# Two SwiGLU layers in fp32 on one core: block 0's last 96 features computed at the end of its block, as a product of seven

## The chip, the core and the metric

The kernel runs on one core of a Trainium2 chip. The metric is the device time of one launch in microseconds; lower is better. All arithmetic is in fp32. TensorE is called PE below, VectorE DVE, ScalarE ACT, GpSimd POOL and SyncE SP, as in the profile.

## The reference

2048 tokens (4 x 512) of width 512 pass two residual layers, each with a layer norm before and after. The first layer keeps, token by token, only the 688 of 1376 gate values that are largest in magnitude.

```python
def layer1(x, w_gate, w_up, w_down):                 # I = 1376, H = 512
    s = silu(x @ w_gate.T)
    s = zero_the_smaller_half_by_abs(s)              # per token, k = I / 2
    return (s * (x @ w_up.T)) @ w_down.T

x = x + layernorm(layer1(layernorm(x), ...))
x = x + layernorm((silu(xn @ W_gate.T) * (xn @ W_up.T)) @ W_down.T)   # xn = layernorm(x)
```

## The kernel before, in words

**Work and stages.** The first layer takes the 16 token tiles of 128 in eight *units* of two tiles (0 to 7). The second layer takes them in four *blocks* of four tiles (0 to 3), with N = 512 tokens a block. Between the layers stand x1 rows in DRAM: each unit's output is normed, added to x and stored there, and a block loads its four tiles again (`Block.norm`: load, layer norm, four transposes on PE, copies to `xT`).

**The second layer's gate and up products.** Of the 1376 features, 1280 are taken in five *groups* (`Block.group`, PE line 849). Each group is a fast bilinear scheme of 26 products of 128x128 by 128x256, whose moving operands are signed sums of `xT` (`Block.sums`, the tiles `T` and `Ts`, 18 additions on DVE, line 277) and whose stationary operands are sums of weights made earlier. The results are gathered from PSUM by DVE (line 859) and ACT (line 863), and POOL multiplies gate by up (line 872).

**The last 96 features.** 1376 is 1280 + 96. For blocks 1 to 3 the gate and up rows of these 96 features are one product of seven (`Block.rest_sevens`, a Strassen-Winograd product over class `Seven`, PE line 210): its left operand is the seven sums `rest_left` of the weights `w_rest`, its right operand the sums `R` of `xT`, which POOL makes in four additions (`Block.rest_right`, lines 193 to 196, tiles `R` with the tag "y"). For block 0 they are computed plainly (`Block.rest`, PE line 881: two outputs, each four matmuls of 128x96 by 128x512), at the change of layers, ahead of the last unit's down product.

**The down product.** `downs` (helper lines 339 to 455) makes it for a pair or two pairs of tiles, in seven products p1 to p7 of five matmuls each (PE line 368), with the last 96 rows as single matmuls into the same banks (line 374). Its weights come as one 640 KB load for each product (`wd_p`, in three buffers). Outputs are gathered in tiles `y` (tag "y", four buffers), normed (`out_norm`: line 170 statistics, line 176 the power -1/2 on POOL, line 486 less the mean, line 488 times the scale plus `xr`), and stored.

**The change of layers.** After unit 7's products the program writes: the down product of units 5 and 6, `blocks[0].norm`, unit 7's search and transposes (`ph`, line 750), `blocks[0].sums()`, `blocks[0].rest`, the down product of unit 7, then the groups of block 0.

**What sets the order.** Every engine executes its own queue in order. The order in the queues is not the written one: a scheduler merges the steps by its own estimate of times when the program is built, and keeps to `tc.issue_after(...)` where that stands. So the order is fixed in the built program, and can be read there for both kernels. Tiles with the same tag share a ring of buffers: a new tile waits until the old one in its buffer has been read and stored. Loads and stores all pass one SP queue in order.

Of the kernel before, what the change touches and what calls it, by code (L numbers as in the profile page):

```python
# [9 lines left out]
F32 = mybir.dt.float32  # L10
BF16 = mybir.dt.bfloat16
I32 = mybir.dt.int32
AF = mybir.ActivationFunctionType
# [3 lines left out]
P = 128  # L17
# [76 lines left out]
def sandwich_kernel(  # L94
# [18 lines left out]
    nc = tc.nc  # L113
    NT, H = x.shape
    I = a_wg.shape[1]
    K = int(0.5 * I)
    assert 2 * K == I
    NH = H // P
# [7 lines left out]
    N = TB * P  # L126
# [3 lines left out]
    HF = HC * P  # L130
# [24 lines left out]
    x1 = dram.tile([NT, H], F32, name="x1")  # L155
# [5 lines left out]
    def bank(tag, nm):  # L161
        return psum.tile([P, 512], F32, tag=tag, name=nm)
# [20 lines left out]
    def stationary_sums(eng, a11, a12, a21, a22, s1, s2, s4):  # L183

        eng.tensor_add(s1, a21, a22)
        eng.tensor_sub(s2, s1, a11)
        eng.tensor_sub(a21, a11, a21)
        eng.tensor_sub(s4, a12, s2)
        return dict(p1=a11, p2=a12, p3=s4, p4=a22, p5=s1, p6=s2, p7=a21)
# [149 lines left out]
        nc.sync.dma_start(t, src)  # L339
        return t  # L340

    def downs(work, pairs, key, w_d, wr, res, dst, nm, final=False):

# [7 lines left out]
        def begin():  # L353
            tiles, left, last = pairs[len(st)]
            pa, px, py = [bank(k, f"{k}d{nm}_{tiles[0]}")[:, :H2] for k in ("pa", "px", "py")]
            ya, yb = [
                work.tile([P, H], F32, tag="y", name=f"y{nm}_{t}", bufs=4) for t in tiles
            ]
            st.append((tiles, left, last, pa, px, py, ya, yb))

# [21 lines left out]
        def p1(i):  # L382
            begin()
            product("p1", PA, i)
# [7 lines left out]
        def p7():  # L392
            product("p7", PX)
            for p in st:
                tiles, left, last, pa, px, py, ya, yb = p
                nc.vector.tensor_add(yb[:, hi], yb[:, lo], px)
                pz.append(bank("pt", f"pz{nm}_{p[0][0]}")[:, :H2])
                rest(pz[-1], p, 1, hi, True)
# [382 lines left out]
                self.tiles, lambda k, c: self.dleft[k][:, c, :], lambda i: self.hT[i][1]  # L781
            )

    def finish(units, wr):

        u = units[0]
        steps = downs(u.work, [u.pair() for u in units], "a", a_wd, wr, x, x1, u.nm)

        def p2():
            steps[-3]()  # L790
            for u in units:
                a12, s2 = u.dleft["p3"], u.dleft["p6"]
                nc.vector.tensor_sub(a12, a12, s2)

        return steps[:-3] + [p2] + steps[-2:]

    class Block:
# [73 lines left out]
                    if not left[f] and not left[2 + f]:  # L871
                        nc.gpsimd.tensor_mul(h[:, part], sg[:, part], h[:, part])  # L872

        def rest(self, w):

            n = I - 2 * HF
            nm = f"{self.nm}_{self.b}"
            ps = [bank(k, f"{k}rb{nm}")[:n, :] for k in ("pa", "px")]
            for c, t in zip(ps, w):
                for k in range(NH):  # L880
                    nc.tensor.matmul(
                        c, t[:, k, :], self.xT[k // 2][:, k % 2, :],
                        start=k == 0, stop=k == NH - 1,
                    )
            h = self.work.tile([P, N], F32, tag="junk", name=f"hTb{nm}_r", bufs=1)
            nc.scalar.activation(h[:n], ps[0], AF.Silu)
            nc.vector.tensor_mul(h[:n], h[:n], ps[1])
            self.hr = h

        def rest_right(self):  # L890

            t = [
                self.work.tile([P, 2, N2], F32, tag="y", name=f"R{self.nm}_{self.b}_{q}", bufs=4)
                for q in range(4)
            ]
            self.right = moving_sums(
                nc.gpsimd,
                *[half[:, :, cols] for half in self.xT for cols in (slice(N2), slice(N2, N))],
                *t,
            )  # L900

        def rest_sevens(self, left):

            n = I - 2 * HF
            nm = f"{self.nm}_{self.b}"
            t = self.work.tile([P, 4, N2], F32, tag="c", name=f"sgr{nm}")[:n]
            m = Seven(f"rb{nm}", left, self.right, t[:, 0, :], t[:, 1, :], t[:, 2, :])
            m.first()
            c11 = m.second()
            h = self.work.tile([P, N], F32, tag="junk", name=f"hTb{nm}_r", bufs=1)  # L910
            lo, hi = h[:n, :N2], h[:n, N2:]
            nc.scalar.activation(lo, c11, AF.Silu)
            m.third()
            nc.scalar.activation(hi, m.c12, AF.Silu)
            nc.vector.tensor_mul(lo, lo, m.c21)
            nc.vector.tensor_mul(hi, hi, m.c22)
            self.hr = h
# [32 lines left out]
    def count_bad():  # L950

        bad = small.tile([P, 1], F32, tag="bad", name="bad", bufs=2)
        nc.vector.tensor_reduce(bad, flags, AX.XY, ALU.add)
        pb = bank("pt", "pbad")
        nc.tensor.matmul(pb[:1, :1], bad, onec, start=True, stop=True)
        badi = const.tile([1, 1], I32, name="badi")
        nc.vector.tensor_copy(badi, pb[:1, :1])
        traced = nc.cur_bb.bb.instructions
        k = len(traced)
        nbad = nc.values_load(badi[0:1, 0:1], min_val=0, max_val=2 * P * NTT)  # L960
        return nbad, [i for i in traced[k:] if i.engine == mybir.EngineType.DVE]

    def layers(nm, general):
        with ExitStack() as sctx:
            wpool = sctx.enter_context(tc.tile_pool(name="w" + nm, bufs=1))
            big = sctx.enter_context(tc.tile_pool(name="big" + nm, bufs=10))
            work = sctx.enter_context(tc.tile_pool(name="work" + nm, bufs=2))

            def last_rows(w_d, layer):
                n = I - 2 * HF  # L970
                w = work.tile([P, H], F32, tag="wr", name=f"wr{layer}{nm}", bufs=1)
                nc.sync.dma_start(w[:n, :], w_d[2 * HF :, :])
                return w[:n, :]

            blocks = [Block(b, nm, big, work) for b in range(NTT // TB)]


            units = [Unit(j, nm, big, work) for j in range(NU)]
# [14 lines left out]
            for q in range(2):  # L993
                b = [
                    wu[:, 2 * r : 2 * r + 2, k * Q : (k + 1) * Q] for r in range(2) for k in (q, 2 + q)
                ]
                t = [y[:, :, ts(q, Q)] for y in (t1, t2, t4)]
                right.append(moving_sums(nc.vector, *b, t[0], t[1], b[1], t[2]))
            nbad = None
            if general:  # L1000
                wr = last_rows(a_wd, 1)
# [13 lines left out]
            else:  # L1015
                wr = last_rows(a_wd, 1)
# [3 lines left out]
                for j in range(NU):  # L1020
                    gate, up = [[] for i in range(6)], [[] for i in range(6)]
                    if j > 2:
                        steps = finish([units[j - 3]], wr)
# [26 lines left out]
                steps = finish(units[-3:-1], wr)  # L1050
# [23 lines left out]
            for tag, n in (("wg", 43), ("wu", 43), ("wus0", 10), ("wus1", 10)):  # L1074
                n = min(n, NG * NP - len(w_of))
                t = wpool.tile([P, n, P], F32, tag=tag, name=f"{tag}2{nm}")
                i = 0
                while i < n:
                    g, j = divmod(len(w_of), NP)
                    k = min(NP - j, n - i)  # L1080
# [3 lines left out]
            n = I - 2 * HF  # L1084
            t = wpool.tile([P, 7, 2, n], F32, tag="wus2", name=f"w_rest{nm}")
            w_rest = [t[:, 2 * q : 2 * q + 2].rearrange("p a b h -> p (a b) h") for q in range(2)]
            for w, w_d in zip(w_rest, (f_wg, f_wu)):
                nc.sync.dma_start(w, w_d[:, 2 * HF :].rearrange("(k p) h -> p k h", p=P))
            w_rests = [t[:, q] for q in range(4, 7)]
            if general:  # L1090
                blocks[0].sums()
            else:
                blocks[0].sums()
                blocks[0].rest(w_rest)
                for f in finish([units[-1]], wr):
                    f()
            wr = last_rows(f_wd, 2)
            for b, block in enumerate(blocks):
                last = b + 1 == len(blocks)
                for a in range(HC):  # L1100
                    block.group(a, w_of[a * NP : (a + 1) * NP])
                    block.down_sums(a)
                    if b == 2 and a == 0 and not general:
                        nbad, loads = count_bad()
                    if b and a == 1:
                        with tc.issue_after(normed[-1]):
                            block.rest_right()
                if b:
                    block.rest_sevens(rest_left)
                elif general:  # L1110
                    block.rest(w_rest)
                if b == 0:
                    blocks_w = [w[:, 2 * c : 2 * c + 2, :] for w in w_rest for c in range(2)]
                    with tc.issue_after(block.mark):
                        rest_left = stationary_sums(nc.vector, *blocks_w, *w_rests)
                if not last:
                    with tc.issue_after(block.mark):
                        for k in range(TB):
                            blocks[b + 1].norm(k)
                    blocks[b + 1].sums()  # L1120
                with ExitStack() as order:
                    if last and not general:
                        for i in loads:
                            order.enter_context(tc.issue_after(i))
                    block.finish([0, 1], wr, last)
# [43 lines left out]
```

## Time and profile before

| What | Value |
|---|---|
| median of 3 runs (lowest to highest) | 848.5 us (848.37 to 850.13) |
| the profiled execution, its time | 848.49 us |
| its span | 846.7 us, 10717 instructions |
| granted TensorE clock over the span | 0.998 |
| DVE busy | 592.4 us (70%) |
| ACT busy | 346.9 us (41%) |
| POOL busy | 178.4 us (21%) |
| DMA moved | 112.20 MB, mean 133 GB/s |

The profiled execution took 1.8 us more than its span and is level with the median. Busy time is what the profiler recorded on an engine; a row of the groups view gives a source line, the engine, the tile names, the count, the busy time and the mean of one. PE's records overlap: a matmul of fp32 leaves two records, which start 0.216 us apart at 256 columns although each lasts 0.379 us. So on PE the distance between starts is what counts. The chain of work that ended last lies on PE for 98% of the span and on DMA for 1%.

### The profile page before, as it was taken

The page shows a single profiled execution, that of the slowest core. Times are in us where ns is not written, and L with a number is a line of the kernel's source. Part 1 is how long each engine was busy: PE and PEld are TensorE (multiplying, and loading weights), DVE is VectorE, ACT ScalarE, POOL GpSimd, SP SyncE. Part 2 cuts the span into 40 slices and gives each one's busy share as a digit, 9 for nine tenths or more (in the row PEclk, how much of TensorE's full clock was granted, in tenths as well). Part 3 has the DMA queues.
Part 4 walks back from the last instruction along what each step waited for, and adds up shares of the span by engine and source line. Part 5 has one row for each costly group of instructions (what it writes and reads, how often), then busy time and mean ns, then how long its engine had stood idle before and what let it go on. Part 6 is the DMA issues. An engine that isn't in the chain of part 4 may idle for free.

```text
span 846.7 us, 10717 instructions
## 1 busy us (share of the span) xinstructions
PE 837.0 (99%) x3544; PEld 641.0 (76%) x3544; DVE 592.4 (70%) x1676; ACT 346.9 (41%) x717; POOL 178.4 (21%) x236
## 2 busy tenths in 40 slices
PE   9999999999999999999999999999999999999996
PEld 5656566767667667677868888888888888888885
DVE  5988769697887949587796665776656666476524
ACT  3356675556557573746321331133211332033300
POOL 1010000000100000000020553074503653075401
PEclk9999999999999999999999999999999999999999
DMA  9996013827424134277557002520055001530032
GB/s 338 385 355 234 1 56 102 278 75 246 137 87 160 56 125 160 71 263 275 183 186 252 1 2 74 200 93 1 2 174 185 8 1 30 205 120 1 1 99 80
DMA packets 65393, 112.20 MB, mean 133 GB/s; under 512 B 4720, under 2 KB 44784, under 8 KB 64432
## 3 DMA queue, kind: packets, MB, share of 16 engines
q1 hardware_dynamic: 65184, 111.16, 38.5%
q8 instruction: 30, 0.49, 0.2%
q14 instruction: 35, 0.29, 0.1%
q10 hardware_dynamic: 144, 0.26, 0.1%
HBM read 90.96 MB, written 20.45 MB: 132 GB/s over the span
## 4 chain that ended last, share of the span: by engine, by line
PE 98%; DMA 1%; DVE 0%; issue 0%; POOL 0%; ACT 0%; POOLq 0%
PE pg L575 18%; PE pab L849 9%; PE pxb L849 9%; PE pyb L849 8%; PE pxu L210 7%; PE pxd L368 6%; PE pxdb L368 6%; PE pyu L210 4%; PE pau L210 4%; PE padb L368 4%; PE pydb L368 4%; PE pad L368 4%; PE pyd L368 4%; PE ph L750 2%; PE pxrb L210 1%; DMA wdb_p<-in_L_ffn_W_down_dram 1%
## 5 line engine op out<-in xcount | busy, mean ns | idle before, releaser
L627 ACT ACTIVATE ja<-v,cur 128x1376 bf16<-128x1376 f32 x96 | 138.4, 1442 | 54.8 <-DVE cur L652 43.6
L575 PE MATMUL pg<-wg,xT 128*128 128x456 f32 (+1 forms) x384 | 155.2, 549 | 0.0
L575 PEld LDWEIGHTS pg<-wg,xT 128*128 128x128 f32 x384 | 72.0, 190 | 61.9 <-issue 57.2
L872 POOL TENSOR_TENSOR hTb<-sg,hTb 128x512 f32<-128x512 f32 x40 | 50.8, 1272 | 96.9 <-DVE hTb L859 90.6
L176 POOL TENSOR_TENSOR rs_o<-ve_o,nhalf 128x1 f32<-128x1 f32 x16 | 14.4, 917 | 181.0 <-DVE ve_o L174 181.0
L579 ACT ACTIVATE p<-pg 128x456 f32<-128x456 f32 (+1 forms) x48 | 26.3, 547 | 58.6 <-PE pg L575 47.9
L176 POOL TENSOR_TENSOR rs_i<-ve_i,nhalf 128x1 f32<-128x1 f32 x16 | 13.2, 829 | 152.8 <-DVE ve_i L174 58.5
L870 ACT ACTIVATE sg<-sg 128x512 f32<-128x512 f32 x40 | 23.0, 621 | 49.0 <-DVE sg L859 49.0
L210 PE MATMUL pau<-wu,xT 128*128 128x344 f32 x128 | 42.7, 452 | 0.0
L859 DVE TENSOR_TENSOR sg<-sg,pxb 128x256 f32<-128x256 f32 x80 | 33.7, 421 | 10.3 <-PE pxb L849 8.3
L859 DVE TENSOR_TENSOR hTb<-hTb,pab 128x256 f32<-128x256 f32 x60 | 25.1, 419 | 22.4 <-PE pab L849 11.0
L368 PE MATMUL padb<-wdb_p,hTb 128*128 128x256 f32 x160 | 38.1, 380 | 0.7 <-DMA wdb_p<-in_L_ffn_W_down_dram 0.7
L368 PE MATMUL pad<-wd_p,hT 128*128 128x256 f32 x160 | 38.6, 379 | 0.0
L863 ACT ACTIVATE hTb<-pab 128x256 f32<-128x256 f32 x40 | 15.3, 384 | 56.1 <-PE pab L849 56.1
L368 PE MATMUL pydb<-wdb_p,D 128*128 128x256 f32 x160 | 37.7, 379 | 0.0
L368 PE MATMUL pxd<-wd_p,hT 128*128 128x256 f32 x160 | 36.8, 379 | 0.0
L368 PE MATMUL pxdb<-wdb_p,hTb 128*128 128x256 f32 x160 | 36.4, 379 | 0.0
L632 DVE TENSOR_SCALAR low<-cur 128x2 int32<-128x2 f32 x48 | 7.9, 164 | 40.7 <-ACT ja L627 40.5
L755 ACT COPY hT<-ph 128x512 f32<-128x512 f32 (+1 forms) x44 | 22.4, 513 | 33.4 <-PE ph L750 29.7
L368 PEld LDWEIGHTS pxd<-wd_p,hT 128*128 128x128 f32 x160 | 30.4, 190 | 5.7 <-issue 0.6
L368 PEld LDWEIGHTS pad<-wd_p,hT 128*128 128x128 f32 x160 | 29.8, 190 | 6.3 <-issue 1.3
L368 PEld LDWEIGHTS padb<-wdb_p,hTb 128*128 128x128 f32 x160 | 30.3, 190 | 5.3 <-DMA wdb_p<-in_L_ffn_W_down_dram 1.1
(304 smaller groups left out, 1938.5 us busy)
## 6 DMA issues: line engine op xcount, KB each, us to landing
wd_p<-sum_a SPq DMA_DIRECT2D x28, 640.0 KB, 3.9
wd_p<-in_L_attn_w_down_dram SPq DMA_DIRECT2D x21, 640.0 KB, 3.8
wdb_p<-sum_f SPq DMA_DIRECT2D x16, 640.0 KB, 4.0
wdb_p<-in_L_ffn_W_down_dram SPq DMA_DIRECT2D x12, 640.0 KB, 4.9
w_ops<-area SPq DMA_DIRECT2D x4, 1664.0 KB, 6.0
xn<-in_x_dram SPq DMA_DIRECT2D x16, 256.0 KB, 4.2
xr<-in_x_dram SPq DMA_DIRECT2D x16, 256.0 KB, 4.7
x<-y SPq DMA_DIRECT2D x16, 256.0 KB, 4.1
```

Of the source, the lines that this page charges most:

```text
L176: nc.gpsimd.tensor_tensor(rs, ve, nhalf, ALU.pow)
L210: nc.tensor.matmul(ps, self.left[k][:, c, :], self.right[k][:, c, :], start=first and c == 0, stop=c == 1, skip_group_check=not first,)
L368: nc.tensor.matmul(p[which], p[1](k, c), ws[k][:, c, :], start=first and c == 0, stop=c == HC - 1, skip_group_check=not first,)
L575: nc.tensor.matmul(pg, self.xT[:, i, c, :], wg[:, c, c0:c1], start=(c == 0), stop=(c == NH - 1),)
L579: nc.scalar.activation(p[:, c0:c1], pg, AF.Silu)
L627: nc.scalar.activation(junk, v, AF.Sign, bias=cur[:, 0, i : i + 1], accum_out=cur[:, 1, i : i + 1],)
L750: nc.tensor.transpose(pt[: isz[i], c, :], h[:, i * P : i * P + isz[i]], ident)
L755: copy(hT[:, g0 : g0 + nf, :], pt[:, :nf, :])
L849: self.product = nc.tensor.matmul(banks[k], w[wv], self.left[xv], start=first, stop=True, skip_group_check=not first,).ins
L859: self.mark = add(c, c, banks[k]).ins
L870: nc.scalar.activation(sg[:, part], sg[:, part], AF.Silu)
L872: nc.gpsimd.tensor_mul(h[:, part], sg[:, part], h[:, part])
```

## The change

Block 0's last 96 features are no longer computed plainly at the change of layers. `Block.rest` is gone, and block 0 takes the way of blocks 1 to 3: the right-hand sums `R` on POOL after group 1, and `rest_sevens` at the end of the block. The weight sums `rest_left`, which DVE made at the end of block 0, are now made during its groups. Since the `R` tiles need the four "y" buffers, the last unit's two `y` tiles are allocated with the tag "xn" (three buffers, otherwise for loaded token tiles).

```diff
-    def downs(work, pairs, key, w_d, wr, res, dst, nm, final=False):
+    def downs(work, pairs, key, w_d, wr, res, dst, nm, final=False, room=("y", 4)):
...
             ya, yb = [
-                work.tile([P, H], F32, tag="y", name=f"y{nm}_{t}", bufs=4) for t in tiles
+                work.tile([P, H], F32, tag=room[0], name=f"y{nm}_{t}", bufs=room[1]) for t in tiles
             ]
...
-    def finish(units, wr):
+    def finish(units, wr, room=("y", 4)):
...
-        steps = downs(u.work, [u.pair() for u in units], "a", a_wd, wr, x, x1, u.nm)
+        steps = downs(u.work, [u.pair() for u in units], "a", a_wd, wr, x, x1, u.nm, room=room)
...
-        def rest(self, w):
...
                 blocks[0].sums()
-                blocks[0].rest(w_rest)
-                for f in finish([units[-1]], wr):
+                for f in finish([units[-1]], wr, ("xn", 3)):
                     f()
...
-                    if b and a == 1:
+                    if a == 1:
                         with tc.issue_after(normed[-1]):
                             block.rest_right()
-                if b:
-                    block.rest_sevens(rest_left)
-                elif general:
-                    block.rest(w_rest)
-                if b == 0:
-                    blocks_w = [w[:, 2 * c : 2 * c + 2, :] for w in w_rest for c in range(2)]
-                    with tc.issue_after(block.mark):
-                        rest_left = stationary_sums(nc.vector, *blocks_w, *w_rests)
+                    if b == 0 and a == 1:
+                        blocks_w = [w[:, 2 * c : 2 * c + 2, :] for w in w_rest for c in range(2)]
+                        with tc.issue_after(block.mark):
+                            rest_left = stationary_sums(nc.vector, *blocks_w, *w_rests)
+                block.rest_sevens(rest_left)
```

## The prediction

> **What bounds the kernel now.** I read the page first: PE is busy for the whole span, so only what lengthens PE's queue or makes it wait can move the time.
>
> ```profile
> PE 837.0 (99%) x3544; PEld 641.0 (76%) x3544; DVE 592.4 (70%) x1676; ACT 346.9 (41%) x717; POOL 178.4 (21%) x236
> ```
>
> Then PE's waits. There are three, and two lie where the change works: a weight load at the end of block 0, and DVE in its first group.
>
> ```profile
> PE warm L150 <- POOL ident masks.py:199: 1.7, 1, 1.7
> PE padb L368 <- DMA wdb_p<-in_L_ffn_W_down_dram: 0.7, 1, 0.7
> PE pxb L849 <- DVE sg L859: 0.2, 1, 0.2
> ```
>
> Third, the groups of PE by shape, for the plain product (line 881) and a product of seven (line 210).
>
> ```profile
> L210 PE MATMUL pxrb<-R,w_rest 128*96 128x256 f32 x36 | 9.2, 379 | 0.0
> L881 PE MATMUL parb<-xTb,w_rest 128*96 128x512 f32 x8 | 3.8, 602 | 0.0
> L881 PE MATMUL pxrb<-xTb,w_rest 128*96 128x512 f32 x8 | 3.8, 592 | 0.0
> ```
>
> Last, PE's timeline (start, duration) at both places. The ends of blocks 0 and 1 first, from the first matmul of the down or rest products to block 1's or 2's first group:
>
> ```profile
> 509.14 1.89 PE L368 MATMUL padb<-wdb_p,hTb 128*128 128x256 f32 x8
> ...
> 532.19 4.58 PE L368 MATMUL padb<-wdb_p,hTb 128*128 128x256 f32 x20 [0.70 <-DMA wdb_p<-in_L_ffn_W_down_dram]
> ...
> 548.27 0.60 PE L849 MATMUL pab<-T,area 128*128 128x256 f32 x2
> ```
>
> ```profile
> 601.80 1.03 PE L210 MATMUL parb<-xTb,w_rest 128*96 128x256 f32 x4
> ...
> 645.87 0.60 PE L849 MATMUL pab<-T,area 128*128 128x256 f32 x2
> ```
>
> And the change of layers, from unit 7's transposes to group 1 of block 0:
>
> ```profile
> 428.22 2.33 PE L750 MATMUL ph<-ident,p 128*128 128x128 f32 x14
> ...
> 462.42 0.70 PE L849 MATMUL pxb<-xTb,area 128*128 128x256 f32 x2 [0.18 <-DVE sg L859]
> ...
> 466.84 0.59 PE L849 MATMUL pab<-T,wg 128*128 128x256 f32 x2
> ```
>
> **The end of block 0: +4.94 us.** In the built program, PE's order at the end of block 0 becomes that of block 1, instruction by instruction, and so does SP's order of the loads there. So block 1 is the row to take: 645.87 - 601.80 = 44.07 us, against 548.27 - 509.14 = 39.13. The difference is seven products of 2 matmuls at 0.43 us (6.04) less the wait for the down weights with its restart (1.1), which block 1 does not have: seven's matmuls cover it. Seven's own operands hide: the four R sums on POOL take 1.27 us each, and the four weight sums about 0.42 us each on DVE now stand in block 0's groups, where DVE is busy 7.3 of 11.2 us. If that cover failed, 4 x 0.42 = 1.7 us would be the price; I take 0.
>
> **The change of layers: PE's work falls by 6.90.** The plain product is 8 matmuls at 0.863 us (four of them fill 437.48 to 440.91 in the timeline). From 428.22 to 466.84 are 38.62 us, of which work: 14 + 4 transposes at 0.108 (1.94), pz 0.43, the plain product 6.90, unit 7's down product (38 matmuls at 0.43: 16.4), group 0 (26 x 0.43: 11.2); in all 36.9, idle 1.7. Without the plain product 30.0 are left, and the question is how much PE then waits; call it S. The sum is 4.94 - (38.6 - 30.0) + S = S - 3.7.
>
> **Working out S.** The plain product needed only what was there, and stood where DVE made the sums T and D for what follows. PE's new order: 3 transposes, four matmuls of p1, 4 transposes, p1's fifth, 7 transposes, product 0, the transposes of block 0's last tile, pz, p5, p6, products 1 and 2, p2, products 3 and 4, p7, 5 to 8, p4, p3, the rest of the group. I lay it against DVE's new order with the durations of the old one (each start 0.08 before the previous end).
> - PE reaches product 0 at 431.90. Its sum on DVE comes after the y sum that starts at 429.89, two statistics of 0.69, an aggregate of 0.17 and one sum of 0.42, and ends at 432.25. Wait 0.4.
> - p5 needs D, the sum of unit 7's transposed tiles (0.79). Ahead of it now stand both mean subtractions (0.48 each): it runs 433.24 to 434.04. PE is ready at 433.71. Wait 0.4.
> - p6 needs the second D. Two residual additions of line 488 (0.75 each) and three T sums (0.34 each, start to start) go first: it ends at 437.12. PE is ready at 436.35. Wait 0.85. The residual additions find their rows of x, issued at 429.70 and 430.66, landed after 3.1 and 3.5 us.
> - p2's load takes the buffer of p5, so it is issued when p5 ends, at 436.5. In the old order p7 and three products lay between; in the new one only p6 and two products: PE is ready at 440.3. Loads of this kind landed after 3.8 to 5.1 us here; the row nearest to it is the same p2's, issued behind an xr load as it will be now:
>
> ```profile
> 443.27 0.38 SPq L339 DMA_DIRECT2D wd_p<-in_L_attn_w_down_dram  x1
> ```
>
> ```profile
> wd_p<-in_L_attn_w_down_dram SPq DMA_DIRECT2D x1, 640.0 KB, 5.1
> ```
>
>   I take 5.1: p2 begins at 441.6, wait 1.3. By 3.8 it would be nothing; by 6.8, the landing behind the wait at 532.19 (issued at 525.32), 3.0.
> - After that the order is covered: p3's load is issued when p7 ends (447.2), is wanted at 451.5 and took 3.8 before. DVE's wait in the group (0.45 with its restart, at 462.42) stays, since unit 7's last norms again stand between the group's additions.
> - Each of the four waits costs some 0.1 more, as the restarts after the old ones do.
>
> S = 0.4 + 0.4 + 0.85 + 1.3 + 0.4 + 0.45 = 3.8. The sum is **+0.1 us**: the 0.9 us of PE work saved and the load wait that is covered at the block's end are given back at the change of layers. On the profiled 848.49 (span 846.7 and 1.8 around it, level with the median) this is 848.6. SP's other move, block 1's token loads behind unit 7's stores, has some 60 us before they are used.
>
> **A rule against it.** POOL's four R sums now wait in its queue ahead of unit 7's two powers (line 176), and their buffers come free when the y rows of units 5 and 6 are stored, near 437 (issued near 434.8, landing 2.1 to 3.3 us). That is amid DVE's T sums, which run to 441.7. Two rows show what such a meeting costs:
>
> ```profile
> 434.57 4.93 POOL L176 TENSOR_TENSOR rs_o<-ve_o,nhalf 128x1 f32<-128x1 f32 x2 [5.79 <-DVE ve_o L174]
> ```
>
> ```profile
> 516.49 0.88 DVE L187 TENSOR_TENSOR w_rest<-w_rest 128x192 f32<-128x192 f32 x1
> ```
>
> In the first POOL stood still while DVE ran sums back to back (its pair takes 1.2 us at 427.61). In the second DVE's sum took twice its 0.44, beside POOL's sums of the down operands. The Trainium skill (SBUF — State Buffer, "SBUF: two separate sides") says that DVE with two SBUF inputs and POOL hold a shared port pair as a lock: whichever starts first has it for the whole instruction. By the first row the R sums wait until DVE's first operand from PSUM near 441.7, then delay only sums that are wanted after 446: price 0. By the rule alone, taking turns, each R sum that slips in delays DVE by 1.27. I take the row, as DVE starts each sum before the last has ended.
>
> **The rivals.**
> - *Slower: POOL gets its turns.* If the R sums enter between T sums from 437.2 on, two stand ahead of product 1's sum (439.0 becomes 441.5) and four ahead of product 3's (441.4 becomes 446.5, wanted at 444.0). PE waits some 2.5 us more: 851.1. It decides from about two R sums before 441; one is hidden behind p2's load. For it: the second row. Against: the first row, in which POOL waited through seven sums, until DVE ran a mean subtraction. Chance 0.18.
> - *Faster: the waits overlap.* If p2 lands after 3.8 us (-1.4 with the restart) and DVE's 0.45 in the group and half of the waits for D go too (-0.9), S is 1.5: 846.3. For it: the loads' median of 3.8. Against: p2 can't begin before p5's end plus the landing, and p5 waits for D. Chance 0.10.
> - My forecast, that waits take the place of the saving: 0.72.
>
> **How the numbers follow.** The forecast alone reaches from 847.2 (landing 3.8) to 850.3 (6.8). The range 847.0 to 850.8 adds part of the slower rival. A difference of 0.2%, 1.7 us, is about what the measurement can tell from none. Faster 0.11 (the faster rival and a little of the forecast), same 0.70, slower 0.19.
>
> **What would show it.** Line 881 is gone; line 210 has 14 more matmuls in block 0, and its end takes about 44.1 us with no wait for the load at p2. From unit 7's transposes to group 1 take about 33.8 us, with PE waiting for DVE before p5 and p6 and for the DMA of p2. R sums of 1.27 us after 441, or stretched ones that began at 437, speak for the row; T sums over 0.5 us for the slower rival. Wrong if that stretch is under 32 or over 35.5 us, or if DVE waits for POOL's powers of unit 7.

## The result, and the profile after

| Kernel | Median | Range, runs | Ratio to before, 95% |
|---|---|---|---|
| before | 848.78 us | 848.37 to 850.13, 4 | |
| after | 855.19 us | 854.12 to 856.49, 4 | 1.0074 [1.0063, 1.0086] |

The change makes the kernel 6.4 us slower; the forecast was 848.6 in a range of 847.0 to 850.8. The profiled execution after took 854.12 us, the fastest of the four (span 852.3 against 846.7, so +5.6). Here are PE's waits after: what waits, on what, then the sum, the times and the longest.

```profile
PE pxd L368 <- DVE D L775: 3.8, 1, 3.8
PE warm L150 <- POOL ident masks.py:199: 1.7, 1, 1.7
PE pab L849 <- DVE hTb L859: 1.6, 1, 1.6
PE pt L508 <- DVE xn L505: 0.5, 1, 0.5
PE pt L514 <- DVE xn L181: 0.5, 1, 0.5
...
```

The wait for `wdb_p` at the end of block 0 is gone, and there are two large new ones: p6 waits 3.8 us for the last unit's D, and a product of group 2 waits 1.6 for DVE. PE's timeline after says where they lie.

```profile
428.78 0.51 PE L750 MATMUL ph<-ident,p 128*128 128x128 f32 x3
...
434.16 2.42 PE L368 MATMUL pyd<-wd_p,D 128*128 128x256 f32 x10
440.37 3.52 PE L368 MATMUL pxd<-wd_p,D 128*128 128x256 f32 x10 [3.79 <-DVE D L775]
...
465.64 0.59 PE L849 MATMUL pab<-T,wg 128*128 128x256 f32 x2
...
481.17 0.70 PE L849 MATMUL pab<-T,wu 128*128 128x256 f32 x2 [1.55 <-DVE hTb L859]
...
509.76 1.03 PE L210 MATMUL parb<-xTb,w_rest 128*96 128x256 f32 x4
...
553.83 0.60 PE L849 MATMUL pab<-T,area 128*128 128x256 f32 x2
```

Three stretches can be read off. The end of block 0 takes 553.83 - 509.76 = 44.07 us, to the last digit what block 1 took before. The change of layers takes 465.64 - 428.78 = 36.86 us, not the 33.8 of the forecast, and more than the 35.5 that the forecast named as its refutation. Group 2 has a wait that was not in it. The difference of the spans adds up: +4.94 at the block's end, -1.76 at the change of layers (36.86 against 38.62), +1.8 in group 2 (the wait and its restart), and some +0.5 of small waits in the first 100 us, together 5.5 of 5.6.

**What stopped p6.** POOL's timeline after, and DVE's in the same microseconds:

```profile
434.15 1.75 POOL L193 TENSOR_TENSOR R<-xTb 128x512 f32<-128x512 f32 x1 [0.36 <-ACT xTb L516]
435.97 1.59 POOL L194 TENSOR_TENSOR R<-xTb,R 128x512 f32<-128x512 f32 x1
438.11 1.53 POOL L195 TENSOR_TENSOR R<-xTb,xTb 128x512 f32<-128x512 f32 x1 [0.55 <-DMA x<-y]
439.63 1.81 POOL L196 TENSOR_TENSOR R<-xTb,R 128x512 f32<-128x512 f32 x1
```

```profile
434.96 1.48 DVE L488 SCALAR_TENSOR_TENSOR y<-y,rs_o,xr 128x512 f32<-128x512 f32 x1 [0.20 <-DMA xr<-in_x_dram]
436.36 1.81 DVE L277 TENSOR_TENSOR T<-xTb,T 128x256 f32<-128x256 f32 x2
...
438.44 1.88 DVE L775 TENSOR_TENSOR D<-D,hT 128x640 f32<-128x640 f32 x1
440.24 1.88 DVE L776 TENSOR_TENSOR hT<-hT,hT 128x640 f32<-128x640 f32 x1
```

Each of the four R sums (1.27 us when alone, as in blocks 1 to 3 of the kernel before) meets one of these DVE rows. Rows of the same kind in the kernel before, and its R sums of line 193 (count, then shortest, median and longest in ns, first and last start):

```profile
435.74 0.82 DVE L775 TENSOR_TENSOR D<-D,hT 128x640 f32<-128x640 f32 x1
436.47 0.82 DVE L776 TENSOR_TENSOR hT<-hT,hT 128x640 f32<-128x640 f32 x1
...
438.34 0.76 DVE L277 TENSOR_TENSOR T<-xTb,T 128x256 f32<-128x256 f32 x2
439.01 0.75 DVE L488 SCALAR_TENSOR_TENSOR y<-y,rs_o,xr 128x512 f32<-128x512 f32 x1
```

```profile
L193 POOL TENSOR_TENSOR R<-xTb x3: 1267/1269/1272, 555.2 to 750.7; 128x512 f32<-128x512 f32 x3
```

After the change the four DVE rows are 0.73, 1.05, 1.06 and 1.06 us longer: 3.9 us of DVE. Each DVE operation that meets an R sum ends only after that sum does (435.90, 437.56, 439.64, 441.44 on POOL). D, line 775, ends at 440.32 where the forecast had 437.12.

**The wait cost more than its length.** The windows view gives, for a stretch: its length, busy time and instructions of PE, PEld, DVE, ACT and POOL, the granted TensorE clock, the DMA share and GB/s. Right after the wait:

```profile
441.90:443.00 1.10, 1.10 (x4) 0.84 (x3) 1.10 (x4) 0.00 (x0) 0.00 (x0) 0.50 0.32 112
```

The clock is at half. From 440.4 to 441.3, with PE already at work again, it was still 1.00. From 441.5 to 445.0 eight records start 0.43 us apart instead of 0.216, which is 1.7 us more.

**What stopped group 2.** The four weight sums on DVE, queued ahead of the evictions of group 2's first products (the additions of line 859, which take a product's result out of PSUM and so free its bank):

```profile
477.40 0.42 DVE L185 TENSOR_TENSOR w_rest<-w_rest 128x192 f32<-128x192 f32 x1
477.85 1.31 DVE L186 TENSOR_TENSOR w_rest<-w_rest 128x192 f32<-128x192 f32 x1
479.09 0.89 DVE L187 TENSOR_TENSOR w_rest<-w_rest 128x192 f32<-128x192 f32 x1
479.90 0.88 DVE L188 TENSOR_TENSOR w_rest<-w_rest 128x192 f32<-128x192 f32 x1
```

Only the first took its 0.42. POOL was at its gate-by-up product and the D sums of group 1 (476.33 to 482.06), and the other three waited for their turns.

### The profile page after: what moved, and what is told of

It is laid out like the page before. It is cut to its first block, busy times and chain, and to the rows that moved or that the text cites. A ratio compares the mean times of both kernels' runs of the same rounds, so it can differ in the third digit from the quotient of the medians.

```text
span 852.3 us, 10747 instructions
## 1 busy us (share of the span) xinstructions
PE 836.9 (98%) x3556; PEld 642.8 (75%) x3556; DVE 598.0 (70%) x1682; ACT 346.6 (41%) x719; POOL 181.7 (21%) x240
## 4 chain that ended last, share of the span: by engine, by line
PE 91%; DVE 4%; SPq 2%; DMA 2%; issue 0%; POOL 0%; POOLq 0%; DVEq 0%
PE pg L575 15%; PE pxb L849 9%; PE pab L849 9%; PE pyb L849 8%; PE pxdb L368 6%; PE pxu L210 6%; PE pxd L368 6%; PE pyu L210 4%; PE pydb L368 4%; PE padb L368 4%; PE pau L210 4%; PE pad L368 3%; PE pyd L368 3%; PE ph L750 2%; PE pxrb L210 1%; DMA area<-in_L_ffn_W_up_dram 1%
## 5 line engine op out<-in xcount | busy, mean ns | idle before, releaser
L176 POOL TENSOR_TENSOR rs_o<-ve_o,nhalf 128x1 f32<-128x1 f32 x16 | 10.8, 690 | 177.4 <-DVE ve_o L174 177.4
L859 DVE TENSOR_TENSOR hTb<-hTb,pyb 128x256 f32<-128x256 f32 x60 | 25.2, 421 | 12.3 <-PE pyb L849 11.8
```

The source lines that it names most:

```text
L176: nc.gpsimd.tensor_tensor(rs, ve, nhalf, ALU.pow)
L859: self.mark = add(c, c, banks[k]).ins
```

## The experiments

Theory at the outset: the loss has two causes of one kind, POOL's R sums among DVE's sums at the change of layers, and DVE's weight sums among POOL's sums at the head of group 2; without both the forecast's own sum should come out. Rival: the buffers, or the change of layers itself, is what costs. In the edits `pmark` is POOL's last product of a group (line 872), so that what is issued after it stands behind it in POOL's queue.

| Run | Median | Ratio to before, 95% |
|---|---|---|
| R sums later | 853.61 us, 6 runs | 1.0055 [1.0041, 1.0069] |
| weight sums on POOL | 855.31, 6 | 1.0064 [1.0049, 1.0079] |
| both moved | 851.34, 5 | 1.0034 [1.0021, 1.0047] |
| before + R sums | 851.95, 5 | 1.0034 [1.0021, 1.0047] |
| before + buffers | 849.22, 13 | 1.0005 [0.9997, 1.0013] |
| both moved, p7 first | 849.47, 13 | 1.0009 [1.0001, 1.0018] |
| and D first | 849.14, 13 | 1.0001 [0.9993, 1.0009] |
| p7 first, additions last | 849.20, 13 | 1.0004 [0.9995, 1.0012] |
| p7 first, additions after all T | 847.76, 13 | 0.9988 [0.9980, 0.9996] |
| the same again | 847.44, 21 | 0.9985 [0.9979, 0.9992] |
| before + additions after all T | 848.93, 22 | 1.0005 [0.9998, 1.0013] |

**R sums later.** Only POOL's order differs from the changed kernel: the R sums stand behind group 1's products.

```diff
-                        with tc.issue_after(normed[-1]):
+                        with tc.issue_after(normed[-1] if b else block.pmark):
                             block.rest_right()
```

> The changed kernel with one thing moved: in block 0 POOL makes the four R sums behind its gate-times-up products of group 1, not during DVE's T and D sums. The orders of the other engines stay the same. Theory (POOL's R sums and DVE's two-operand sums keep each other off shared SBUF ports): the second D of unit 7 takes about 0.8 us and not 1.88, PE waits for it under 1.2 us and not 3.8, its clock is not halved afterwards, and from unit 7's transposes to group 1 it takes about 33.8 us and not 36.9: 855.2 - 3.1 = 852.1 us, with the wait of 1.55 us in group 2 still there. Rival (DVE's own new order, with two residual additions ahead of that D, makes it late, and POOL is off the path): 855 us, the wait stays.

Measured: 853.61 us. In its profile p6's wait falls from 3.8 to 0.6 and the clock stays whole (0.998 over the span), but p2 now waits 2.0 us for its load, which p6's delay had hidden, and group 2's wait is 2.1. PE's idle time from 428 to 470 (the distance between starts beyond a matmul's own 0.216 us, the half clock included) falls from 6.9 to 4.8 us, the median by 1.6, half of what was expected: the collision is real, and part of what it gave back went into the next wait.

**Weight sums on POOL.** Only they move, from DVE's queue to POOL's, behind group 2's products.

```diff
-                    if b == 0 and a == 1:
+                    if b == 0 and a == 2:
...
-                        with tc.issue_after(block.mark):
-                            rest_left = stationary_sums(nc.vector, *blocks_w, *w_rests)
+                        with tc.issue_after(block.pmark):
+                            rest_left = stationary_sums(nc.gpsimd, *blocks_w, *w_rests)
```

> The changed kernel with the four weight sums of the last 96 features made on POOL behind its products of group 2, instead of on DVE ahead of group 2's additions. Theory (they took 0.42 to 1.31 us on DVE beside POOL's sums, and held group 2's first additions up): the wait of 1.55 us at group 2 goes, 855.2 - 1.8 = 853.4 us; the wait of 3.8 us before p6 and the half clock stay. Rival (group 2 waits for something else, such as a buffer of the group's outputs on POOL): 855 us or more.

Measured: 855.31 us, no gain in the median, which is the rival's number. But group 2's wait is gone in the profile, so the weight sums were its cause, and not a buffer. The profiled execution, the slowest of the six (852.0 to 856.0), lost elsewhere: it waited 1.6 us at product 0 (for the reason given under *p7 first*) and 4.9 at p6, and from within that wait on the clock was at half for 6.8 us. By itself this run doesn't settle what the weight sums cost; next to the following one it does.

**Both moved.**

> The changed kernel with both moved, the R sums behind group 1 and the weight sums to POOL behind group 2. Theory: both waits go and with them the half clock. The prediction's own sum should then hold: 849 to 850 us, level with the kernel before or up to 0.15% above it. Rival (the change of layers has a third loss that these waits hide): over 851 us, with new waits of PE between 430 and 466 us.

Measured: 851.34 us, 3.9 below the changed kernel. It is 2.3 below the first run, which is what moving the weight sums gives once the R sums are out of the way, and 4.0 below the second, which is the same for the R sums: both collisions are real. But it is still 2.5 us above before, not the 849 to 850 of the theory, so the rival is right that they are not all. PE's timeline of this run shows the rest:

```profile
438.15 2.43 PE L368 MATMUL pxd<-wd_p,D 128*128 128x256 f32 x10 [1.50 <-DVE D L775]
...
443.14 2.42 PE L368 MATMUL pad<-wd_p,hT 128*128 128x256 f32 x10 [1.69 <-DMA wd_p<-in_L_attn_w_down_dram]
```

These are the forecast's own waits, larger: p6 1.5 (0.85 forecast) because a row of x landed 0.8 us late for DVE, and p2 1.7 (1.3) because its load was issued late and landed late. SP's timeline has the issue:

```profile
437.27 0.49 SPq L339 DMA_DIRECT2D wd_p<-in_L_attn_w_down_dram  x1
```

That is 0.8 us after the 436.5 of the forecast: in SP's queue the load stands behind the store of the row that DVE finished late (issued at 436.42) and a load of x (436.83). It then took 5.8 us to land and not 5.1. So the late row is paid for at both waits. PE's idle time from 428 to 470 is 5.2 us, S of the forecast 3.8.

**The R sums alone, and the buffers alone.** The kernel before, plain product and all, with R made (and not used) and the last unit's y tiles in "xn"; then with the y tiles alone.

```diff
-                for f in finish([units[-1]], wr):
+                for f in finish([units[-1]], wr, ("xn", 3)):
...
-                    if b and a == 1:
+                    if a == 1:
                         with tc.issue_after(normed[-1]):
                             block.rest_right()
```

> The kernel before with only the R sums of block 0 added on POOL, unused, and with unit 7's y tiles in the xn buffers; the plain product stays at the change of layers. Theory: the R sums stretch DVE's sums as in the changed kernel, by 3 to 4 us in all, but the plain product's 6.9 us of matmuls cover it, so the time stays within 0.1%: 848.8 us. The loss then needs both, the sums that collide and the cover taken away. Rival (what collides costs wherever it stands): 852 us.

> The kernel before with one part of the change alone: the last unit's two y tiles in the buffers of the tag xn; the plain product and everything else stay. In the built program only SP's order of the loads of token tiles (xnb) moves, by a few places. My theory: these buffers are free, so 848.8 us, within 0.1% of before, and what the run of the R sums alone lost (3.1 us) is all due to the R sums meeting DVE. Rival: part of that loss is the buffers' own (a token tile of block 0 or 1 arrives later because its buffer is taken): then this kernel is at 850 or more and PE shows a wait for xnb or xn between 428 and 470.

Measured: 851.95 with the R sums, a miss for my theory that the plain product would cover them; 849.22 with the buffers alone, which can't be told from before. So the R sums cost 2.5 to 2.7 us (by the ratios, by the medians) even where PE has 6.9 us of other work. How they get past that cover, in PE's timeline with the R sums (the profiled execution is the slowest of the five, 854.01 us):

```profile
449.24 1.22 PE L849 MATMUL pxb<-T,area 128*128 128x256 f32 x2 [2.30 <-DVE hTb_r L887]
```

The delay ran through DVE's queue to the last of these sums, the eviction of the plain product, whose PSUM bank product 1 wanted. Not all of this one wait is the R sums': the token tile discussed under *p7 first* came late in this execution too (DVE waited 4.0 us for it, 2.3 in the profile before). That the R sums cost something doesn't rest on it: all five runs (851.15 us or more) lie above all eleven of the kernel before beside them (850.17 or less).

**p7 first.** To the run with both moved is added that p2's matmuls stand behind p7's on PE, so that p7 and four products cover p2's load.

```diff
+                    with tc.issue_after(p7s[-1]) if k == "p2" and p7s else ExitStack():
+                        m = nc.tensor.matmul(p[which], p[1](k, c), ws[k][:, c, :],
...
+                    if k == "p7" and room[0] == "xn": p7s.append(m.ins)
```

> The changed kernel with the R sums and the weight sums moved as in the run with both moved (851.3 us), and in addition p7 of the last unit ahead of its p2 on PE, so that four products of group 0 and p7 (some 6 us of PE work with p6) lie between p5's end, which frees p2's buffer, and p2. My theory: what is left of the loss sits in two waits of the change of layers, p2's load (1.9 us there) and p6's operand D (1.7). Then the wait for wd_p is gone or under 0.3 us and the time is 849.3 to 849.7, with the wait for D still at some 1.7. Rival: the loads are bound by the rate at which data comes, or the order of the group is what costs, so the wait moves on to p7, p4 or to the group's additions, and the time stays at 851.0 to 851.6.

Measured: 849.47, as my theory had it. The wait for `wd_p` is gone. The profile has no wait for D either, which the theory had left at 1.7, but only because PE lost the time earlier. Product 0 waited, and p5 then ran at half clock (10 records in 4.04 us, not 2.42), so that D was ready at its end:

```profile
433.82 0.70 PE L849 MATMUL pab<-T,area 128*128 128x256 f32 x2 [1.63 <-DVE T L277]
```

DVE's waits from 400 to 432 in the same run tell why:

```profile
DVE st_ib L170 <- DMA xnb<-x: 3.8, 1, 3.8
```

DVE had lost its time some 25 us earlier, waiting for a token tile of block 0. In the profiles of this study that wait is 1.8 to 2.7 us or 3.5 to 4.0. Where it was the longer, product 0 (where no plain product stood ahead) waited 1.4 to 1.7 us; where the shorter, at most 0.5. No run moved that load by itself. The kernel before has 6.9 us of plain product behind that point.

**D first.** In addition DVE makes D ahead of the last two residual additions of units 5 and 6: these are held back as closures in `ends` and issued after line 776.

```diff
+                with tc.issue_after(units[-1].dmark):
+                    for f in ends: f()
```

> As the run with p7 ahead of p2, and in addition DVE makes the sums D of the last unit ahead of the last two residual additions of units 5 and 6 (line 488), which wait for rows of x. My theory: D_1 ends near 436.1 instead of 438.1, p6 follows p5 without a wait of note (0.3 at most), and both waits are gone: 847.4 to 848.0, some 0.1% below the kernel before, which is the saved PE work at last on the clock. Rival (waits move on): DVE is itself behind at this place, so product 1 waits for its T sums instead and the time stays within 0.5 us of the run with p7 first alone.

Measured: 849.14, only 0.3 lower by the medians (0.7 by the ratios, whose intervals overlap). This is the rival's case: p6 does not wait, but products 1 and 3 wait for T sums that the additions now delay (0.2 and 1.3 us).

**Additions last, and additions after all T sums.** The same two additions are held back further: first behind the T sum that is written last, then behind all 18.

```diff
-                with tc.issue_after(blocks[0].tmark): [f() for f in ends]
+                with ExitStack() as o:
+                    for i in blocks[0].tmarks: o.enter_context(tc.issue_after(i))
+                    for f in ends: f()
```

> As the run with p7 ahead of p2, but the last two residual additions of units 5 and 6 (line 488, 1.4 us together) now stand in DVE's queue behind all T sums of block 0, where DVE has room (16.4 of 24 us busy from 446 to 470). Theory: from 428 to 444 the change of layers is bound by DVE, which runs there without a gap, so every DVE instruction ahead of what PE wants there is paid in full. Then the waits for T and Ts in front of products 1 and 3 (0.2 and 1.3 us in the run with D first) go, and the time is 847.4 to 848.2, below that run's 849.1. Rival: DVE's work as a whole is the bound, so the additions delay the evictions of the first products behind them and PE waits there for a bank as long: 848.9 to 849.4.

> As the run with the additions last, but with the two residual additions truly behind all 18 T sums of block 0: in that run they stood ahead of the T sum that was written last but not queued last, and PE waited 1.0 us for a Ts. PE's order is unchanged. Theory: this wait goes, and the time is 847.9 to 848.5, some 0.1% under that run's 849.2 and level with the kernel before or a little below it. Rival: DVE's work as a whole is the bound, so the evictions of the first products (line 859), now behind the additions, keep PE waiting for a bank as long: 849.0 to 849.4.

Measured: 849.20, a miss; the additions landed in front of the last *queued* T sum, which isn't the last written one, and product 4 waited 1.0 us for it, so the theory was not yet tested. With the second edit 847.76 (below the 847.9 to 848.5 of the theory), which is under both kernels. Its PE timeline and then the windows of its change of layers, followed by the same window of the kernel before:

```profile
433.52 0.70 PE L849 MATMUL pab<-T,area 128*128 128x256 f32 x2 [0.50 <-DVE T L277]
...
441.16 0.67 PE L849 MATMUL pab<-Ts,area 128*128 128x256 f32 x2 [0.48 <-ACT sg L863]
...
461.40 0.59 PE L849 MATMUL pab<-T,wg 128*128 128x256 f32 x2
```

```profile
428.00:444.00 16.00, 14.87 (x79) 12.26 (x78) 16.00 (x46) 5.28 (x14) 3.02 (x4) 1.00 0.75 247
```

```profile
428.00:444.00 16.00, 15.84 (x63) 9.49 (x62) 14.68 (x37) 4.43 (x12) 5.71 (x4) 1.00 0.65 215
```

The third busy column is DVE: 16.00 of 16.00 us here, 14.68 in the kernel before. The stretch from unit 7's transposes (they begin at 429.11 here) to group 1 is 461.40 - 429.11 = 32.29 us, 2.3 of it idle.

**Is it the change, or the additions?** The kernel before with the additions behind all T sums, beside the last kernel once more.

> The kernel before, with the plain product, and only one thing: the two residual additions of units 5 and 6 stand behind all T sums of block 0 on DVE, as in the run that was a little faster than the kernel before. My theory: in the kernel before PE has 6.9 us of plain product to do while DVE makes its sums, so it does not wait for them (its waits at the change of layers come to 1.7 us, 0.45 of it in the group): nothing to win, 848.4 to 849.0. Rival: the gain of that run (0.95 us) is the additions' own and has nothing to do with the plain product: 847.7 to 848.0.

> The kernel with the two additions behind all T sums once more, beside the kernel before with that edit alone, on one chip. If the change itself is worth something once its waits are gone: 847.5 to 848.1, 0.1% below its neighbour. If the gain was the additions' own: level with its neighbour.

Measured: 848.93 (no gain) and 847.44. Moving the additions brings nothing where the plain product covers DVE; even the lowest of these 22 runs (848.00) is not below the lowest of before (847.55). It can cost something there: the profiled execution took 852.18 us, as p2's load was issued behind the stores of the two late tiles (at 444.85, before at 443.27) and landed after 7.4 us (5.1), PE waited 2.6 us for it, and the clock fell to half. The other moves can't be the gain either: the kernel before makes no R sums for block 0, PE waits for none of its weight sums, and its p7 is ahead of p2 already (446.53 and 448.68). So the change is worth 1.3 us (0.15%; 0.12% in the first run) against the kernel before once R sums, weight sums, p7 and the additions are moved; as it was made it costs 6.4.

## Why the prediction was wrong, step by step

- **The end of block 0, +4.94: right.** 44.07 us, no wait at p2.
- **PE's work at the change of layers, -6.90: right.** The work of 30.0 us and PE's idle time of 6.9 give the measured stretch of 36.9.
- **R "ready near 437" and price 0: the step that failed.** It had two parts. The R sums began at 434.15: the first two found buffers that were already stored, and waited only for the last copy to `xT`, so they met the sums up to unit 7's D and the D sums themselves, and not the T sums of products 1 and 3. And they did not wait for DVE. Price 0 became the largest part of the miss: p6 waited 3.8 us and not 0.85, and the clock took 1.7 more; p2's wait of 1.3 then fell away, as its load had landed by the time. With smaller differences that is the 3.1 us by which the stretch exceeds the 33.8 of the forecast. I had set the row of POOL standing still (434.57 before) above the rule of the Trainium skill (SBUF — State Buffer, "SBUF: two separate sides"), that whichever side starts first holds the shared ports for its whole instruction. The runs decide for the rule: by it four sums delay DVE by up to 4 x 1.27 = 5.1 us (an estimate), measured 3.9. The row showed one side of a lock that goes either way, which is how I read the runs together. In the run of the R sums alone both stand in one trace: a POOL power held up for 3.96 us at 438.91, and from 443.43 on an R sum beside which a DVE addition takes 1.75 instead of 0.75. My reading is that POOL gets in at a gap of DVE (0.20 us before 434.96, waiting for a row of x) and that the two then take turns; no run here tried that by itself.
- **The slower rival had the mechanism, not the place or size.** It put the R sums at 437 and 2.5 us at products 1 and 3. It was 3.8 us at p6, where three R sums stand ahead of D's end (0.73 + 1.05 + 1.06 = 2.8 us), and 1.7 more for the clock. The mark it named, T sums over 0.5 us, is there: one of the two at 436.36 took 1.5.
- **The clock was left out.** After p6's wait of 3.8 us the granted clock was 0.5 for 3.4 us, which cost 1.7. The Trainium skill (TensorE: Matmul & The Clock Gate, "Part 1: The HAM clock gate (the "warmup" mystery)") has PE drop to half rate after an idle window of about 3.4 us that runs freely of the program. By it the forecast's waits, none over 1.3 us, cost no clock, and a wait of 3.8 us may. The rule isn't the whole story here: the clock fell only 1.2 us after PE had begun again, and half clock followed waits of 2.6 us (before with the additions moved), 2.3 (R sums alone) and 1.6 (p7 first) too, but not waits of 1.3 to 2.1 us in four other profiles.
- **Weight sums, "4 x 0.42 = 1.7 would be the price; I take 0": the cover failed.** DVE's 7.3 of 11.2 us was an average of the group. The sums stood at its head, ahead of evictions that PE wants at once, and beside POOL's sums three of them took 0.9 to 1.3 us. PE lost 1.8 us with the restart, close to the price of 1.7 that the forecast had named and set aside.
- **S = 3.8: right in kind, small in size.** With both collisions moved it is 5.2: p6 loses 0.8 and p2 0.6 us more than forecast (restarts included).
- **What the sum had not seen: DVE becomes the bound of that stretch.** I worked out waits one by one. From 428 to 444 DVE had hardly a gap. Putting p7 first brought 1.9 us, but D first only 0.3, as the next wait for DVE stood behind it. Moving DVE's own work out of the stretch, from ahead of the last T sum to behind it, brought 1.4 (849.20 to 847.76).

Open: small waits of 0.2 to 0.7 us each elsewhere, which come and go between profiles; what makes the token tile of block 0 land late; what makes the clock fall after one wait of 1.6 us and not after another; and what decides whether POOL or DVE has its turn.

## What to carry to other kernels

Taking work off the bounding engine can be worth nothing in a stretch where another engine is as busy; look at both engines' busy time in that window, not over the span, before counting on the saving. Work moved to a second engine is paid for where its operands' ports or queue meet the first: find the microsecond at which it can start (the first buffer that is free, not the last) and who is then at work. A saving that comes out as nothing can still be had by moving out of the stretch what nobody is waiting for there.

## What was not expected of the hardware

- DVE and POOL sums with two operands in SBUF behaved here as if they took turns by whole instructions: 0.75 and 0.82 us on DVE become 1.48 and 1.88, 1.27 on POOL becomes 1.5 to 1.8. A small DVE sum of 128x192 suffers as much (0.42 to 1.31).
- PE's clock fell to half for 3.4 us after waits of only 1.6, 2.3 and 2.6 us in three profiles; where it ran through all of that, such a wait cost 1.7 us more than its length.
- The landing of one token tile of block 0 differed by 1.5 us between executions, and where it was late product 0 waited over 1 us longer some 25 us after.
